# A layer of chunked attention and gated FFN on one core: the first blocks' start, block 1 by seven products, and the order of the head

## The chip, the cores and the metric

The kernel runs on one core of a Trainium2 chip. The core has five engines that this text names by the profile's letters: PE (TensorE, matrix products), DVE (VectorE), ACT (ScalarE), POOL (GpSimd) and SP (SyncE, which here only issues transfers). Matrix products are written to PSUM, which the kernel uses as eight banks of 128 x 512 floats; everything else lives in SBUF. The metric is the device time of one execution in microseconds (us), the median over several runs.

## The reference

The input x is 4 sequences of 2048 tokens of 256 features, 8192 tokens in all. Cut to what matters:

```python
# attention, in chunks of 32 tokens
Q, K, V = x @ W_q.T, x @ W_k.T, x @ W_v.T
S = einsum(Qc, Kc) * mask          # inside each chunk; mask[i, j] = decay**(i-j), i >= j
O = einsum(S, Vc)
a = (sigmoid(x @ W_g.T) * O) @ W_o.T + x
h = layernorm(x + a)
# FFN, weights are integers times 1/127, hidden width 768
f = (silu(h @ wg.T) * (h @ wu.T)) @ wd.T
out = layernorm(h + f)
```

Both layer norms are without weights, with an epsilon of 1e-5.

## The kernel before, in words

**Blocks.** The tokens are worked on in 16 blocks of 512 (`NB`, `TB`). For each block the attention part makes a gate `sg`, a product `y = x M` (with M = W_q^T W_k made once in `make_m`, L188, so that scores need one projection instead of two), values `v`, masked scores `sT`, gated values `goT`, and the output projection plus twice x (the kernel halves wo instead, `HALF`), which is then normalised to `h`. The FFN part makes gate and up products of six chunks of 128 hidden features (`ffn_up`, banks `fg` and `fu`) and the down product (`ffn_down`, bank `fdn`), with each operand split in a high part (fp32r) and a low part (f16). The two parts are software-pipelined: the loop at L934 runs the FFN of block b beside the attention of blocks b+2 and b+3. What comes before that loop, the attention of blocks 0 and 1 and the beginning of block 2, is called the head here (L892 to L922).

**Dense and by sevenths.** A product of the attention part can be made in two ways. The dense way (`attn_gate` L560, `attn_y` L576, `attn_v` L592, and `project_back` L658 under `attn_out` L694) multiplies the whole operands: 8 block products of half size. The other way (`seven`, L482) is a Strassen-type scheme that needs only 7 products of half size, of sums of quarters: products 1, 6, 5 and 7 go to four banks, the additions are made from them by ACT, DVE and POOL, and in a second call (`rest`) products 2, 3 and 4 are accumulated onto the banks of 1, 5 and 7, and the four quarters of the result are put together. The sums of quarters of a weight are made once by POOL (`weight_sums` L423, five operations), those of an activation for each block (`token_sums` L436, four operations; for x, and for `goT` ahead of the output). `split_gate`, `split_v`, `split_y` and `split_out` are the four products in this way. In the kernel before, blocks 2 to 15 use the sevenths (but for the last block's output); blocks 0 and 1 are dense.

**Layer norm.** There are three forms. `layer_norm` (L322) takes the moments (DVE), a square root (ACT, a function that needs another table than the sigmoid), a reciprocal and four normalising operations (DVE). In the loop `scale_and_shift` (L348) and `normalize` (L404) do the last part on ACT, four activations with a scale and a shift. `iterated_scale_and_shift` (L364) has no square root of ACT: three small operations on DVE give a first guess and twelve small ones on POOL improve it; before, only the last blocks use it.

**From h to its transpose.** Block 0's h is transposed on PE (`transpose_h`, L712). For later blocks `move_h` (L731) makes four 32-square transposes on DVE and lets SP issue 16 transfers that put the squares in place, and `split_h` (L754) makes the high and low parts of the result (ACT and POOL) for the next iteration's FFN.

**The order.** The program is written in the order of the Python text, and a scheduler may reorder within an engine; `in_turn`, and `in_steady_turn` inside the loop, keep an operation in its place. Waits follow from the data and from the buffers: most work tiles have two buffers, PSUM has eight banks, and a bank is free again when its reader has read it.

**The start.** At the beginning SP and ACT issue the loads: wg, wv, wk and wo from ACT's queue, the two halves of xT_0, then wq, xT_1, the x blocks and the nine integer pieces of the FFN weights from SP's (`load_w` L129, `load_xT` L117). Meanwhile PE multiplies a tile of zeros (`idle`, L174 to L178), DVE builds the decay mask (L213 to L236), and POOL the identity and zeroed score tiles. Later in the head ACT casts the FFN's integers to their high and low parts (`integers`, L244, 18 casts of 128x512), and DVE finds each piece's largest integer (`look_up`, L260), five pieces in the head and four in iteration 0; a path for wider integers is compiled behind a test and isn't run with these inputs.

The order of the head before:

```python
    sg, v = attn_gate(0), attn_v(0)
    make_m()
    sg_1 = attn_gate(1)
    yT = attn_y(0)
    look_up(range(5))
    v_1 = attn_v(1)
    ...
```

Of the kernel before, what the change touches and what calls it, by code (L numbers as in the profile page):

```python
# [67 lines left out]
WARM = 2  # L68
# [3 lines left out]
def kernel(  # L72
# [36 lines left out]
    def bank(name):  # L109
        return psum.tile([P, TB], F32, tag="ps", name=name)  # L110
# [18 lines left out]
    def load_w(eng, w, name):  # L129
        k, n = w.shape[0] // P, w.shape[1]  # L130
        t = const.tile([P, k, n], w.dtype, tag=name, name=name)
        eng.dma_start(t, w.rearrange("(k p) n -> p k n", p=P))
        return t
# [5 lines left out]
    wg = load_w(nc.scalar, w_gT, "wg")  # L139
# [5 lines left out]
    wo = load_w(nc.scalar, w_oT, "wo")  # L145
# [28 lines left out]
    idle = const.tile([P, TB], F32, tag="idle", name="idle")  # L174
    nc.vector.memset(idle, 0.0)
    pi = bank("pi")
    for _ in range(WARM):
        nc.tensor.matmul(pi, lhsT=idle[:, :P], rhs=idle, start=True, stop=True)  # L178
# [9 lines left out]
    def make_m():  # L188
        pm = bank("pm")
        for ec in range(KD):  # L190
            for dc in range(KD):
                nc.tensor.matmul(
                    pm[:, ec * D : (ec + 1) * D],
                    lhsT=wq[:, dc, ec * P : (ec + 1) * P],
                    rhs=wk[:, dc, :],
                    start=(dc == 0),
                    stop=(dc == KD - 1),
                )
        nc.vector.tensor_copy(m_sb.rearrange("p k n -> p (k n)"), pm)
# [122 lines left out]
    def layer_norm(r, name, on_r=1.0, on_dst=1.0):  # L322


        mv = moments(r, name)
        rstd = root(mv, name, on_r)
        nc.vector.reciprocal(rstd, rstd)
        if on_dst != on_r:
            nc.vector.tensor_scalar(rstd, rstd, on_dst / on_r, None, ALU.mult)
        for g in range(NG):  # L330
            nc.vector.tensor_scalar(
                r[:, g, :],
                r[:, g, :],
                mv[:, g, 0:1],
                rstd[:, g : g + 1],
                ALU.subtract,
                ALU.mult,
            )
# [221 lines left out]
    def attn_gate(b):  # L560
        xt = xTs[b]
        sg = work.tile([P, KD, TB], F32, tag="sg", name=f"sg_{b}")
        for dc in range(KD):
            pg = bank(f"pg_{b}_{dc}")
            for ec in range(KD):
# [6 lines left out]
                )  # L572
            nc.scalar.activation(sg[:, dc, :], pg, AF.Sigmoid)
# [317 lines left out]

    hs, hTs = {}, {}  # L892
    sg, v = attn_gate(0), attn_v(0)
    make_m()
    sg_1 = attn_gate(1)
    yT = attn_y(0)
    look_up(range(5))
    v_1 = attn_v(1)
    in_turn(nc.scalar.mul(wo, wo, HALF))
    fg = integers(ffn_gT, ffn_int[0], "fg")  # L900
    fu = integers(ffn_uT, ffn_int[1], "fu")
    fd = integers(ffn_dT, ffn_int[2], "fd")
    sT = attn_scores(0, yT)
    for w, name in ((wv, "v"), (m_sb, "m"), (wg, "g")):
        w_sums[name] = weight_sums(w, name)
    xTs[2] = load_xT(2)
    x_sums = token_sums(xTs[2], "x_2")
    yT = attn_y(1)
    goT = attn_values(0, sT, v, sg)
    sT_1 = attn_scores(1, yT)  # L910
    w_sums["o"] = weight_sums(wo, "o")
    xTs[3] = load_xT(3)
    hs[0] = attn_out(0, goT)
    v, rest = split_v(2, x_sums)
    goT = attn_values(1, sT_1, v_1, sg_1)
    rest()
    yT, rest = split_y(2, x_sums)
    hs[1] = attn_out(1, goT)
    hTs[0] = transpose_h(0, hs[0])
    rest()  # L920
    sg, g_rest = split_gate(2, x_sums)
# [5 lines left out]
    scales_h = scales_out = r_out = None  # L927
    table = const.tile([P, 1], F32, tag="table", name="table")
# [5 lines left out]
    for b in range(NB - 2):  # L934
# [10 lines left out]
        moving = move_h(b + 1, hs[b + 1])  # L945
# [8 lines left out]
        ffn_up(b, hT, uT, range(2, 3))  # L954
        if not more:
            normalize(r_before, *scales_out)
            store(b - 2, r_before)
# [260 lines left out]
```

## Time and profile before

| quantity | value |
|---|---|
| runs of the kernel before | 533.03, 533.13, 533.16 us (median 533.13) |
| the profiled execution | 532.91 us |
| its span, first to last instruction | 531.1 us |
| granted TensorE clock, mean | 0.996 |
| PE instructions in the span | 3610 matmul records |
| DVE, ACT, POOL busy | 73%, 60%, 62% of the span |
| transfers | 36.90 MB, mean 69 GB/s; 253 GB/s in the first of the 40 slices |

How to read it. The profiled execution is one run, 0.22 us below the median. Its span leaves out 1.8 us around the first and the last instruction. An engine is busy from the start to the end of an instruction; the page puts these together by line and operation, and for the matmuls, which overlap, the end is modelled. A PE stage is best read from the chain of waits, whose pieces follow on one another without overlap: each has a start and a length, then the engine, the bank it writes, the line, and how many records it holds. A 32-bit matmul leaves two records, so 8 records are four matmuls. In the timeline the number in brackets is the idle time just ahead of an instruction on its engine, and after the arrow what ended it.

### The profile page before, as it was taken

How to read it: one execution, taken by the hardware profiler on the slowest of the kernel's cores; microseconds unless marked ns; L12 is line 12 of the kernel's file. 1: busy time of each engine (PE TensorE's matmuls, PEld its weight loads, DVE VectorE, ACT ScalarE, POOL GpSimd, SP SyncE). 2: the span in 40 equal slices, each digit the busy share in tenths (PEclk: the TensorE clock that was granted, in tenths of full speed). 3: DMA queues.
4: the chain of work that ended last, by engine and by line, in shares of the span. 5: the costliest groups of instructions: out<-in, count | busy, mean ns of one | idle time of the engine just before them, and what ended most of it. 6: DMA issues, size and time to landing. Idle time of an engine off the chain costs nothing.

```text
span 531.1 us, 10442 instructions
## 1 busy us (share of the span) xinstructions
PE 518.6 (98%) x3610; PEld 418.4 (79%) x3610; DVE 389.3 (73%) x972; ACT 317.0 (60%) x630; POOL 331.2 (62%) x465
## 2 busy tenths in 40 slices
PE   8999999999999999999999999999999999999983
PEld 5588887887978788887878888788797878877753
DVE  4669787686786867777686777868678686788664
ACT  2284566465656656565576666656565665766553
POOL 5231775667848668585766848577684866644562
PEclk9999999999999999999999999999999999999998
DMA  7541210213212131231313113131221312021111
GB/s 253 184 119 39 51 69 25 58 44 79 79 36 85 52 108 41 51 109 30 92 49 113 42 40 102 37 101 41 61 100 32 89 54 69 1 73 47 41 39 44
DMA packets 43128, 36.90 MB, mean 69 GB/s; under 512 B 4672, under 2 KB 38976, under 8 KB 43072
## 3 DMA queue, kind: packets, MB, share of 16 engines
q1 hardware_dynamic: 41952, 35.15, 22.6%
q10 hardware_dynamic: 1088, 1.05, 0.6%
q8 instruction: 30, 0.49, 0.4%
q14 instruction: 26, 0.21, 0.1%
q0 software_dynamic: 32, 0.00, 0.0%
HBM read 20.45 MB, written 8.39 MB: 54 GB/s over the span
## 4 chain that ended last, share of the span: by engine, by line
PE 91%; DVE 3%; POOL 2%; ACT 2%; issue 1%; DVEq 0%; ACTq 0%
PE fg L781 15%; PE fu L781 14%; PE fdn L668 13%; PE p_v L470 8%; PE p_y L452 8%; PE p_g L452 8%; PE p_o L470 8%; PE po L642 5%; PE ps L621 3%; PE pa L668 2%; PE py L582 1%; PE pg L566 1%; PE pv L601 1%; POOL u_lo L806 1%; PE fdn L1079 1%
## 5 line engine op out<-in xcount | busy, mean ns | idle before, releaser
L806 POOL TENSOR_TENSOR u_lo<-u,u_hi 128x512 f16<-128x512 f32 (+1 forms) x98 | 122.9, 1255 | 117.3 <-ACT u_hi L805 115.7
L805 ACT CAST u_hi<-u 128x512 fp32r<-128x512 f32 (+1 forms) x98 | 59.7, 609 | 65.0 <-DVE u L803 64.7
L791 DVE SCALAR_TENSOR_TENSOR s<-fg,s 128x512 f32<-128x512 f32 (+1 forms) x98 | 66.4, 678 | 37.6 <-ACT s L789 37.2
L789 ACT ACTIVATE s<-fg 128x512 f32<-128x512 f32 (+1 forms) x98 | 56.1, 584 | 40.6 <-PE fg L781 40.5
L803 DVE TENSOR_TENSOR u<-fu,s 128x512 f32<-128x512 f32 (+1 forms) x98 | 66.6, 679 | 11.0 <-POOL u_lo L806 1.0
L781 PE MATMUL fg<-hT_hi,fg_hi 128*128 128x512 f32 (+1 forms) x196 | 74.1, 459 | 0.3 <-DVE s L791 0.3
L781 PE MATMUL fu<-hT_hi,fu_hi 128*128 128x512 f32 (+1 forms) x196 | 60.6, 390 | 0.3 <-DVE u L803 0.3
L781 PE MATMUL fg<-hT_lo,fg_lo 128*128 128x512 f16 (+1 forms) x196 | 57.9, 377 | 0.2 <-DVE s L791 0.2
L781 PE MATMUL fu<-hT_lo,fu_lo 128*128 128x512 f16 (+1 forms) x196 | 57.4, 375 | 0.4 <-DVE u L803 0.4
L668 PE MATMUL fdn<-fd_hi,u_hi 128*128 128x256 f32 x312 | 45.7, 288 | 0.0
L781 PEld LDWEIGHTS fu<-hT_hi,fu_hi 128*128 128x128 f32 x196 | 36.5, 188 | 8.9 <-DVE u L803 0.5
L781 PEld LDWEIGHTS fg<-hT_hi,fg_hi 128*128 128x128 f32 x196 | 34.6, 189 | 9.4 <-DVE s L791 0.5
L407 ACT ACTIVATE h<-h,shift_h,scale_h 128x256 f32<-128x256 f32 x52 | 27.0, 589 | 22.6 <-POOL shift_h L358 22.6
L668 PEld LDWEIGHTS fdn<-fd_hi,u_hi 128*128 128x128 f32 x312 | 38.9, 189 | 0.3
L668 PE MATMUL fdn<-fd_lo,u_lo 128*128 128x256 f16 x312 | 38.6, 273 | 0.0
L781 PEld LDWEIGHTS <-fu_lo 128*128 128x128 f16 x196 | 19.2, 98 | 22.8 <-issue 0.6
L764 POOL TENSOR_TENSOR hT_lo<-hT,hT_hi 128x512 f16<-128x512 f32 x28 | 35.2, 1279 | 1.2 <-ACT hT_hi L763 1.2
L829 DVE SCALAR_TENSOR_TENSOR r<-fdn,h 128x512 f32<-128x512 f32 x30 | 20.7, 689 | 20.6 <-PE fdn L668 18.1
L781 PEld LDWEIGHTS <-fg_lo 128*128 128x128 f16 x196 | 15.3, 98 | 21.3 <-issue 13.3
L668 PEld LDWEIGHTS <-u_lo 128*128 128x128 f16 x312 | 28.5, 98 | 3.9
L642 PE MATMUL po<-sT,v 128*128 128x128 f32 x256 | 31.2, 275 | 0.0
L642 PEld LDWEIGHTS po<-sT,v 128*128 128x128 f32 x256 | 30.0, 192 | 0.6 <-issue 0.5
(202 smaller groups left out, 1159.5 us busy)
## 6 DMA issues: line engine op xcount, KB each, us to landing
x<-in_x_dram SPq DMA_DIRECT2D x16, 512.0 KB, 3.6
xT<-in_xT_dram SPq DMA_DIRECT2D x15, 512.0 KB, 4.3
out_dram<-r SPq DMA_DIRECT2D x15, 512.0 KB, 4.0
hT<-sq SPq DMA_DIRECT2D x224, 32.0 KB, 1.9
fg_int<-in_ffn_gT_dram SPq DMA_DIRECT2D x3, 256.0 KB, 7.9
fu_int<-in_ffn_uT_dram SPq DMA_DIRECT2D x3, 256.0 KB, 7.0
fd_int<-in_ffn_dT_dram SPq DMA_DIRECT2D x3, 256.0 KB, 6.0
xT<-in_xT_dram SPq DMA_DIRECT2D x2, 256.0 KB, 4.2
```

The lines of the kernel that those rows point to most:

```text
L407: nc.scalar.activation(r[:, g, :], r[:, g, :], AF.Identity, bias=shift[:, g : g + 1], scale=scale[:, g : g + 1],)
L452: nc.tensor.matmul(pb, lhsT=a[i - 1], rhs=b[i - 1], start=first, stop=True, skip_group_check=True,)
L470: nc.tensor.matmul(pb[:, g * P : (g + 1) * P], lhsT=b[i - 1][:, g * P : (g + 1) * P], rhs=a[i - 1], start=first and g == 0, stop=True, ski ...
L642: nc.tensor.matmul(po[:, cols], lhsT=v[:, g, dc * P : (dc + 1) * P], rhs=sT[:, cols], start=True, stop=True,)
L668: nc.tensor.matmul(pb[:, j * D : (j + 1) * D], lhsT=part[:, g * P : (g + 1) * P], rhs=w, start=(i == 0), stop=(i == len(terms) - 1),)
L764: nc.gpsimd.tensor_tensor(in_order[1], whole, in_order[0].bitcast(F32), ALU.subtract)
L781: nc.tensor.matmul(pb, lhsT=w[kind][:, dc, hc * P : (hc + 1) * P], rhs=hT[kind][:, dc, cols], start=(kind == kinds[0] and dc == 0), stop=( ...
L789: order(nc.scalar.activation(s, pg, AF.Sigmoid, scale=SCALE / H_UP))
L791: gated = nc.vector.scalar_tensor_tensor(s, pg, U_UP / H_UP**2, s, ALU.mult, ALU.mult)
L803: in_steady_turn(nc.vector.tensor_tensor(u, pu, s, ALU.mult))
L805: nc.scalar.copy(hi, u)
L806: nc.gpsimd.tensor_tensor(lo, u, hi.bitcast(F32), ALU.subtract)
```

## The change

All of it lies in the head and in iteration b = 0; the code of later iterations issues what it issued before.

- Start: wg is loaded in two transfers, one for each half of the contracted dimension, and `attn_gate` runs over that dimension in its outer loop, with both banks open. wo is loaded from SP's queue, after xT_1. The warm-up is seven matmuls of 128x128 in place of two of 128x512, and the zero tile is 128x128.
- Block 1's gate, y, v and output are made by `split_gate`, `split_y`, `split_v` and `split_out`. So POOL makes the weight sums of wg and wv, the sums of x_1, and the sums of M and of wo early, and the sums of block 1's goT for its output. wo is halved earlier.
- M is copied out of PSUM by ACT rather than DVE.
- The casts of the FFN weights stand at three places of the head rather than at one.
- h_1 is scaled by `iterated_scale_and_shift`, and normalised by ACT after chunk 2 of iteration 0; its move follows there, rather than at the start of that iteration.
- The sigmoid's table is asked for by an activation of its own after block 0's transposes. `layer_norm` takes an argument that is not used.

```diff
--- before.py
+++ after.py
@@ -65,7 +65,7 @@
 EPS = 1e-5
 U_UP = 2.0**-3
 HALF = 0.5
-WARM = 2
+WARM = 7
 
 
 @with_exitstack
@@ -126,23 +126,26 @@
         nc.sync.dma_start(xn, x[span(b, start), :].rearrange("(g p) d -> p g d", p=P))
         return xn
 
-    def load_w(eng, w, name):
-        k, n = w.shape[0] // P, w.shape[1]
-        t = const.tile([P, k, n], w.dtype, tag=name, name=name)
-        eng.dma_start(t, w.rearrange("(k p) n -> p k n", p=P))
+    def load_w(eng, w, name, pieces=1):
+        n_k, n = w.shape[0] // P, w.shape[1]
+        t = const.tile([P, n_k, n], w.dtype, tag=name, name=name)
+        src = w.rearrange("(k p) n -> p k n", p=P)
+        per = n_k // pieces
+        for k in range(0, n_k, per):
+            eng.dma_start(t[:, k : k + per, :], src[:, k : k + per, :])
         return t
 
 
     decay = const.tile([P, 1], F32, tag="decay", name="decay")
     nc.gpsimd.dma_start(decay, log_decay[0:1, 0:1].to_broadcast([P, 1]))
     xTs, xns = {}, {}
-    wg = load_w(nc.scalar, w_gT, "wg")
+    wg = load_w(nc.scalar, w_gT, "wg", pieces=KD)
     xTs[0] = load_xT(0, pieces=KD)
     wv = load_w(nc.scalar, w_vT, "wv")
     wq = load_w(nc.sync, w_q, "wq")
     wk = load_w(nc.scalar, w_k, "wk")
     xTs[1] = load_xT(1)
-    wo = load_w(nc.scalar, w_oT, "wo")
+    wo = load_w(nc.sync, w_oT, "wo")
     xns[0] = load_xn(0)
     xns[1] = load_xn(1)
 
@@ -171,11 +174,11 @@
     ]
 
 
-    idle = const.tile([P, TB], F32, tag="idle", name="idle")
+    idle = const.tile([P, P], F32, tag="idle", name="idle")
     nc.vector.memset(idle, 0.0)
-    pi = bank("pi")
+    pi = bank("pi")[:, :P]
     for _ in range(WARM):
-        nc.tensor.matmul(pi, lhsT=idle[:, :P], rhs=idle, start=True, stop=True)
+        nc.tensor.matmul(pi, lhsT=idle, rhs=idle, start=True, stop=True)
 
     ident = const.tile([P, P], F32, tag="ident", name="ident")
     make_identity(nc, ident)
@@ -196,7 +199,7 @@
                     start=(dc == 0),
                     stop=(dc == KD - 1),
                 )
-        nc.vector.tensor_copy(m_sb.rearrange("p k n -> p (k n)"), pm)
+        nc.scalar.copy(m_sb.rearrange("p k n -> p (k n)"), pm)
 
 
 
@@ -319,10 +322,10 @@
         )
         return std
 
-    def layer_norm(r, name, on_r=1.0, on_dst=1.0):
-
-
-        mv = moments(r, name)
+    def layer_norm(r, name, on_r=1.0, on_dst=1.0, mv=None):
+
+
+        mv = moments(r, name) if mv is None else mv
         rstd = root(mv, name, on_r)
         nc.vector.reciprocal(rstd, rstd)
         if on_dst != on_r:
@@ -560,9 +563,9 @@
     def attn_gate(b):
         xt = xTs[b]
         sg = work.tile([P, KD, TB], F32, tag="sg", name=f"sg_{b}")
-        for dc in range(KD):
-            pg = bank(f"pg_{b}_{dc}")
-            for ec in range(KD):
+        banks = [bank(f"pg_{b}_{dc}") for dc in range(KD)]
+        for ec in range(KD):
+            for dc, pg in enumerate(banks):
                 nc.tensor.matmul(
                     pg,
                     lhsT=wg[:, ec, dc * P : (dc + 1) * P],
@@ -570,6 +573,7 @@
                     start=(ec == 0),
                     stop=(ec == KD - 1),
                 )
+        for dc, pg in enumerate(banks):
             nc.scalar.activation(sg[:, dc, :], pg, AF.Sigmoid)
         return sg
 
@@ -889,43 +893,51 @@
 
 
 
+    table = const.tile([P, 1], F32, tag="table", name="table")
     hs, hTs = {}, {}
     sg, v = attn_gate(0), attn_v(0)
+    w_sums["g"] = weight_sums(wg, "g")
+    w_sums["v"] = weight_sums(wv, "v")
+    x_sums = token_sums(xTs[1], "x_1")
     make_m()
-    sg_1 = attn_gate(1)
+    w_sums["m"] = weight_sums(m_sb, "m")
+    in_turn(nc.scalar.mul(wo, wo, HALF))
+    w_sums["o"] = weight_sums(wo, "o")
+    sg_1, g_rest = split_gate(1, x_sums)
+    fg = integers(ffn_gT, ffn_int[0], "fg")
     yT = attn_y(0)
     look_up(range(5))
-    v_1 = attn_v(1)
-    in_turn(nc.scalar.mul(wo, wo, HALF))
-    fg = integers(ffn_gT, ffn_int[0], "fg")
+    g_rest()
+    v_1, rest = split_v(1, x_sums)
     fu = integers(ffn_uT, ffn_int[1], "fu")
+    sT = attn_scores(0, yT)
+    xTs[2] = load_xT(2)
+    rest()
+    yT, rest = split_y(1, x_sums)
+    goT = attn_values(0, sT, v, sg)
+    rest()
     fd = integers(ffn_dT, ffn_int[2], "fd")
-    sT = attn_scores(0, yT)
-    for w, name in ((wv, "v"), (m_sb, "m"), (wg, "g")):
-        w_sums[name] = weight_sums(w, name)
-    xTs[2] = load_xT(2)
+    hs[0] = attn_out(0, goT)
+    sT_1 = attn_scores(1, yT)
+    xTs[3] = load_xT(3)
     x_sums = token_sums(xTs[2], "x_2")
-    yT = attn_y(1)
-    goT = attn_values(0, sT, v, sg)
-    sT_1 = attn_scores(1, yT)
-    w_sums["o"] = weight_sums(wo, "o")
-    xTs[3] = load_xT(3)
-    hs[0] = attn_out(0, goT)
     v, rest = split_v(2, x_sums)
     goT = attn_values(1, sT_1, v_1, sg_1)
+    go_sums = token_sums(goT, "go_1")
     rest()
     yT, rest = split_y(2, x_sums)
-    hs[1] = attn_out(1, goT)
+    hs[1], out_rest = split_out(1, go_sums)
     hTs[0] = transpose_h(0, hs[0])
+    in_turn(nc.scalar.activation(table, eps, AF.Sigmoid))
     rest()
+    scales_h = iterated_scale_and_shift(out_rest(), of_h, "h_1")
     sg, g_rest = split_gate(2, x_sums)
     ahead = yT, v, sg
 
 
 
 
-    scales_h = scales_out = r_out = None
-    table = const.tile([P, 1], F32, tag="table", name="table")
+    scales_out = r_out = None
 
     def back_to_sigmoids():
 
@@ -942,7 +954,7 @@
         steady = b > 0
         if b:
             normalize(hs[b + 1], *scales_h)
-        moving = move_h(b + 1, hs[b + 1])
+            moving = move_h(b + 1, hs[b + 1])
         ffn_up(b, hT, uT, range(0, 1))
         if b == 0:
             g_rest()
@@ -952,6 +964,10 @@
         if m + 1 < NB:
             xTs[m + 1] = load_xT(m + 1)
         ffn_up(b, hT, uT, range(2, 3))
+        if b == 0:
+
+            normalize(hs[b + 1], *scales_h)
+            moving = move_h(b + 1, hs[b + 1])
         if not more:
             normalize(r_before, *scales_out)
             store(b - 2, r_before)
```

## The prediction

> **What bounds the kernel now.** I read the page first: busy shares, slices, the chain that ended last.
>
> ```profile
> PE 518.6 (98%) x3610; PEld 418.4 (79%) x3610; DVE 389.3 (73%) x972; ACT 317.0 (60%) x630; POOL 331.2 (62%) x465
> PE   8999999999999999999999999999999999999983
> PE 91%; DVE 3%; POOL 2%; ACT 2%; issue 1%; DVEq 0%; ACTq 0%
> ```
>
> TensorE is busy 98% of the span; only the first slice and the last two fall short. So the time is the sum of the matmuls plus the start and the tail. The change touches only the head, so I asked for PE's waits in the first 85 us.
>
> ```profile
> PE pi L178 <- DVE idle L175: 1.5, 1, 1.5
> ```
>
> That is the only one, before the warm-up. After it no matmul of the head waits: a matmul removed here is a matmul saved, and a new wait costs in full. The chain of waits of the first 80 us prices each stage (start, length):
>
> ```profile
> 1.46 3.58 PE pi L178 x4
> 5.04 0.02 issue
> 5.06 3.70 PE pg L566 x8
> ...
> 12.22 1.73 PE pm L192 x8
> 13.94 3.43 PE pg L566 x8
> 17.38 3.51 PE py L582 x8
> 20.89 3.45 PE pv L601 x16
> 24.34 1.08 PE ps L621 x32
> 25.42 3.63 PE py L582 x8
> ...
> 42.21 3.45 PE pa L668 x16
> ...
> 47.83 1.73 PE p_g L452 x8
> ...
> 51.36 1.29 PE p_g L452 x6
> ...
> 57.53 1.78 PE p_v L470 x16
> ...
> 61.11 1.34 PE p_v L470 x12
> ```
>
> The reader sees a dense stage at about 3.44 us (the second py shows 3.63, behind the narrow score products; I take 3.44 for it as for the others) beside the same stage by sevenths: 1.73 + 1.29 = 3.02 where tokens stay in the columns (gate, y) and 1.78 + 1.34 = 3.12 where they are rows (v, out). The start, from the timeline (start, length, engine; in brackets the idle time and what ended it):
>
> ```profile
> 5.06 0.30 PEld L566 LDWEIGHTS pg<-xT,wg 128*128 128x128 f32 x2 [1.40 <-DMA wg<-in_w_gT_dram]
> ```
>
> The first real matmul waited for wg. The answer on DMA issues (queue, KB, us to landing):
>
> ```profile
> wg<-in_w_gT_dram ACTq DMA_DIRECT2D x1, 256.0 KB, 4.3
> ```
>
> Issued at 0.74, wg landed at 5.04; the first half of xT_0, issued at 0.75, took 3.7 and landed at 4.45.
>
> [...] passes of 128x512 take 0.86 us from 1.46 to 5.04 and 0.43 soon after. [...]
>
> **The change part by part.** Changed lines of DVE, ACT and POOL count only where PE comes to wait for them, and the order from iteration 0 on is the old one, so what the head gains or loses reaches the end one to one.
>
> Sevenths for block 1. Gate 3.43 − 3.02 = 0.41; y 3.44 − 3.02 = 0.42; v 3.45 − 3.12 = 0.33; out 3.45 − 3.12 = 0.33. Sum −1.49 us. Into the bargain, py's 0.07 above 3.44 (it waited a little for m_sb behind DVE's 16 mask copies, 13.43 to 16.41) goes, since ACT, idle there, copies m_sb about 2 us earlier: −0.07.
>
> Start. wg in halves with the ec loop outside lets two matmuls begin on half of wg and half of xT_0. The half of wg is not in the trace; bounds are 5.04 (no gain) and 4.45, below which xT_0 holds it up. I take 4.47, as half of the bytes come first in an otherwise idle queue: 5.06 − 4.47 = −0.59. The warm-up must not be in the way: 7 matmuls are 14 passes of 0.86 / 4 = 0.215, 3.0 us; from about 1.12 (the memset is a quarter of 0.48) to 4.15. Before, it ended only at 5.04, so undoing the load alone would give nothing.
>
> Clock. If the full clock comes at the same moment as now (about 5.1), the 0.6 us of matmul begun early run at half speed and 0.3 is given back; if it comes with activity, nothing. The warm-up also ends 0.3 before work begins. I take +0.1 (0 to 0.3).
>
> wv. It is now third in ACT's DMA queue instead of second. On each queue the third load of before moved nothing until about 2.1 us after the first had landed; if that is a matter of loads, wv lands at 7.6 to 8.7, if of bytes at 6.5 as before. The v matmuls want it at 4.47 + 3.5 = 8.0: 0 to 0.7, I take +0.2. wk (fourth, wanted at 11.4, 9.55 before) and wo (on SP, landing near 12.1, halved by ACT and wanted by POOL after 14) have room.
>
> New waits. I laid the new order of each engine on the durations of the trace. PE order after the gate of block 0: v, m, four gate products of block 1 (13.3), y of block 0, three gate products, four v products, scores of block 0, and so on.
> - Gate products 6, 5, 7 need POOL's x_1 sums: xT_1 lands at 11.43, three sums of 0.73 end near 13.7, product 6 is due at 13.7: 0 to 0.2, I take 0.
> - The last v product of block 1 needs p57_v from DVE, which stands behind five top reduces of 0.62 = 3.1 us begun near 19.4 and block 0's mask products; due 23.95, free about 24.1: +0.15 (0 to 0.5). Behind the waiting product stand the y products.
> - Values of block 1 need their masked scores while DVE still normalises h_0 (1.38): +0.1 (0 to 0.4).
> - Output of block 1: goT comes late from DVE for the same reason, then POOL makes three sums of 0.73 = 2.2 us; PE has 1.34 + 1.73 + 0.44 = 3.5 us to cover goT and sums: +0.25 (0 to 0.9).
> - x_3 sums on POOL stand behind the rooting by iteration. Its price is in the tail of before, which does the same:
>
> ```profile
> 488.57 0.20 POOL L371 TENSOR_TENSOR t_out<-y_out 128x4 f32<-128x4 f32 x1 [0.39 <-DVE y_out L389]
> 488.85 0.20 POOL L371 TENSOR_TENSOR t_out<-t_out,v_out 128x4 f32<-128x4 f32 x1
> ```
>
>   one step each 0.28, eleven dependent ones 3.0 us. The v products of block 3 come three FFN chunks later: +0.1 (0 to 0.6).
> - In iteration 0 ACT normalises h_1 after chunk 2, as in the later loop:
>
> ```profile
> 83.21 2.08 ACT L407 ACTIVATE h<-h,shift_h,scale_h 128x256 f32<-128x256 f32 x4 [2.05 <-POOL shift_h L358]
> 51.16 1.42 DVE L739 STREAM_TRANSPOSE sq<-h 128x256 f32<-128x256 f32 x4
> ```
>
>   2.08 us on ACT ahead of the sigmoid of chunk 3, and the four transposes stop DVE until it is done. Cover on PE is the four v products and chunk 3's 1.8 us; slack about 0.2. I take 0 (0 to 0.95).
> Sum of waits +0.6 (0 to about 3.3).
>
> Hidden at no cost. Layer norm's four DVE operations for h_1 (1.38) go, covered before by PE anyway. Casts in three pieces are the same 18 x 0.55 us of ACT; fg comes first at block 0's y, fd only before the out stage, and FFN wants all near 49, so there are over 5 us left. The table loads are as many (two). SP: hT_1 is moved some 7 us later; its 16 DMAs took 11.4 + 1.9 us, so it lands near 74.7 and PE wants its split near 80.4; if that cover went, each us late would cost one. What is late next when the dense matmuls go is DVE and POOL in block 1's head, which is the list above.
>
> Sum: −1.49 − 0.07 − 0.59 + 0.1 + 0.2 + 0.6 = −1.25. From the profiled execution's 532.91 us (span 531.1 and 1.8 around it) that gives 531.66; the median of the runs is 533.13, 0.22 above the profiled one, so 531.9.
>
> **Rivals.** Times are on the median's scale.
> - A, forecast: 531.9 (531.3 to 532.4 by the mid values).
> - D, all hidden: waits, clock and wv at nothing: 533.13 − 2.15 = 531.0. For it: no wait at all in the head of before. Against: DVE's five reduces sit in the way.
> - B, given back: the start gains nothing, for instance since wg's first half or the clock come as late as now (+0.6), wv costs 0.7 and the waits 0.9: −1.56 + 1.6, 533.1. [...] This is also the case in which the change does not do what it says: the load in halves starts nothing earlier.
> - C, slower: the chain in iteration 0. POOL's 3.0 us of rooting delays the normalise, ACT's 2.08 delay the sigmoid, DVE stands at the transposes, and PE runs out of free banks at chunk 3. Price: 2.08 + 1.42 less 0.2 of slack, 3.3 us; from 531.9 to 535.2, and some 534.7 if half a us is hidden. It decides from a wait of 1.25 us on over no change, and of 2.3 on for a clear loss. For it: three engines in series with a slack of 0.2. Against: the later iterations carry the same normalise at their start, and the longest single wait of PE on another engine after the head is 0.5 us.
>
> **How the numbers follow.** Chances: A 0.42, D 0.15, B 0.25, C 0.18. A measurement tells about 0.2% (1.07 us) from no change. Faster by more: all of D and 0.35 of A, 0.50. Within: 0.07 of A and 0.23 of B, 0.30. Slower: C and 0.02 of B, 0.20. The range for 8 in 10 runs from D's near end, 530.8, into C, 534.5; A's own is 531.3 to 532.4.
>
> **What would show it.** In the changed trace: the first pg near 4.47 and the warm-up over by 4.2; the pg passes at 0.43 from about 5.1; the first pv right behind pg; block 1's stages at 3.0 to 3.1 us each; PE waits for x_sums, p57_v, go_sums of some tenths; and none at chunk 3 of iteration 0. Wrong would make it: a first pg at 5.0, a gap ahead of pv, or a PE wait over 1 us with ACT's normalise or POOL's rooting behind it.

## The result, and the profile after

The changed kernel takes 533.59 us (median of 22 runs, 532.94 to 535.15). Beside it the kernel before was run 22 times and has a median of 532.53 us (531.59 to 533.26), so the three runs shown ahead of the change were on the high side of its spread. The ratio is 1.0021, with a 95% interval of 1.0014 to 1.0027: the change makes the kernel 1.1 us slower. The forecast was 1.25 us faster.

The page of the changed kernel shows the same picture as before, a full PE. The columns are busy time, share and instructions of each engine.

```profile
PE 520.6 (98%) x3656; PEld 425.3 (80%) x3656; DVE 395.3 (74%) x981; ACT 322.4 (61%) x644; POOL 344.7 (65%) x492
PE   8999999999999999999999999999999999999985
```

PE is busy 2.0 us longer than before although the edits take 1.5 us of matmuls out. The head's waits of PE, after the change, for 0 to 90 us (total, times, longest):

```profile
PE pi L181 <- DVE idle L178: 1.1, 1, 1.1
PE p_o L473 <- POOL go_sums L446: 0.8, 1, 0.8
PE pv L605 <- DMA wv<-in_w_vT_dram: 0.6, 1, 0.6
PE p_v L473 <- DVE p_v L508: 0.3, 1, 0.3
PE p_g L455 <- DVE p_g L508: 0.2, 1, 0.2
```

There were none below the first line before. To see where the time goes, the run is cut at points that both kernels have: the first matmul of M, the first of the FFN, the last operation of DVE, the end. First PE's timeline of the kernel before (start, length; the length overlaps the next line by some 0.15):

```profile
12.05 1.89 PE L192 MATMUL pm<-wk,wq 128*128 128x256 f32 x8
...
49.21 0.81 PE L781 MATMUL fg<-hT_hi,fg_hi 128*128 128x512 f32 x2
```

and of the kernel after:

```profile
4.21 4.21 PE L569 MATMUL pg<-xT,wg 128*128 128x512 f32 x8
9.03 3.72 PE L605 MATMUL pv<-wv,xT 128*128 128x256 f32 x16 [0.62 <-DMA wv<-in_w_vT_dram]
12.59 1.89 PE L195 MATMUL pm<-wk,wq 128*128 128x256 f32 x8
...
20.71 0.67 PE L455 MATMUL p_g<-x_sums,g_sums 128*128 128x256 f32 x2 [0.20 <-DVE p_g L508]
...
26.10 0.71 PE L473 MATMUL p_v<-v_sums,x_sums 128*128 128x128 f32 x4 [0.34 <-DVE p_v L508]
...
43.82 1.60 PE L473 MATMUL p_o<-o_sums,go_sums 128*128 128x128 f32 x12 [0.81 <-POOL go_sums L446]
...
50.31 0.81 PE L785 MATMUL fg<-hT_hi,fg_hi 128*128 128x512 f32 x2
```

The last DVE operation starts at 524.87 before and 527.34 after; the spans are 531.1 and 531.4.

| stretch | before | after | difference |
|---|---|---|---|
| start to the first matmul of M | 12.05 | 12.59 | +0.54 |
| to the first FFN matmul | 37.16 | 37.72 | +0.56 |
| to the last DVE operation | 475.66 | 477.03 | +1.37 |
| to the end | 6.19 | 4.09 | −2.10 |

Four things, then, where the prediction had one sum: the start lost time although PE began 0.85 us earlier; the head lost time although it has 1.5 us less to multiply; the loop, in which no instruction was changed after iteration 0, lost 1.4; and the last stores were quicker. The profiled run of before lay 0.4 above its median and that of after 0.4 below, so the spans of the traces differ by 0.4 and the medians by 1.06.

The loop's share is in one stage. The down product of block 1 in the chain of waits (start, length), first before, then after:

```profile
108.91 5.43 PE fdn L668 x48
```

```profile
110.13 5.53 PE fdn L672 x48
```

In the iteration laid side by side stage for stage (from 181 us on) no other stage differs by more than 0.01. The groups by form, 80 to 470 us, give the mean of one in ns after the comma, first before, then after:

```profile
L668 PE MATMUL fdn<-fd_hi,u_hi 128*128 128x256 f32 x298 | 43.8, 288 | 0.0
L668 PE MATMUL fdn<-fd_lo,u_lo 128*128 128x256 f16 x300 | 37.1, 273 | 0.0
```

```profile
L672 PE MATMUL fdn<-fd_hi,u_hi 128*128 128x256 f32 x306 | 45.9, 292 | 0.0
L672 PE MATMUL fdn<-fd_lo,u_lo 128*128 128x256 f16 x302 | 37.5, 273 | 0.0
```

Each high part takes 4 ns longer, the low parts take the same. With 24 high parts in a block that is 0.09 us, in 14 iterations 1.3 us. No wait shows there: it is the matmul itself. What had moved is where the operands lie: the change allocates `table`, 4 bytes in a slot of 32, ahead of the FFN's weights instead of behind them. So fd_hi, a multiple of 64 bytes into the partition before, is 32 bytes past one after. The instructions of the loop and their order are the same. Another difference between the two traces can be set aside: the changed kernel's has 3.4 us at half clock near the end (from 517.3 us), but a second trace of it without that, e13 below, takes 477.00 us from the first FFN matmul to the last DVE operation, where this one takes 477.03.

The head's delays begin on DVE. The 16 mask copies, before (from the timeline of DVE):

```profile
13.43 2.98 DVE L236 COPY mask<-chunk_mask 32x32 f32<-32x32 f32 x16
```

and after:

```profile
14.67 5.10 DVE L239 COPY mask<-chunk_mask 32x32 f32<-32x32 f32 x16
```

They are the same copies, 0.19 apart before and 0.32 after. POOL was idle from 11.0 to 17.2 before; after, it makes the sums of x_1, M and wo between 11.4 and 19.5, with a pause of 0.8 us. The mask is finished 3.4 us later, and the additions of block 1's gate, y of block 0, the five top reduces and the additions of block 1's v all stand behind it in DVE's order.

The start and the head are therefore not two separate sums. In e13, the changed kernel run once more, wv came later still and M began at 13.64 instead of 12.59; but PE then met DVE's additions ready, the waits at p_g and p_v were gone, and the first FFN matmul began at the same 50.31.

### The profile page after: what moved, and what is told of

It is laid out like the page before. It is cut to its first block, busy times and chain, and to the rows that moved or that the text cites. A ratio compares the mean times of both kernels' runs of the same rounds, so it can differ in the third digit from the quotient of the medians.

```text
span 531.4 us, 10605 instructions
## 1 busy us (share of the span) xinstructions
PE 520.6 (98%) x3656; PEld 425.3 (80%) x3656; DVE 395.3 (74%) x981; ACT 322.4 (61%) x644; POOL 344.7 (65%) x492
## 4 chain that ended last, share of the span: by engine, by line
PE 86%; DVE 7%; POOL 2%; ACT 2%; issue 1%; DMA 1%; DVEq 0%; ACTq 0%; POOLq 0%
PE fg L785 15%; PE fu L785 14%; PE fdn L672 14%; PE p_o L473 8%; PE p_y L455 8%; PE p_v L473 8%; PE p_g L455 8%; PE po L646 5%; PE ps L625 3%; PE pa L672 1%; DMA decay<-in_log_decay_dram 1%; POOL u_lo L810 1%; PE fdn L1095 1%; DVE mask L239 1%; ACT r L410 1%
## 5 line engine op out<-in xcount | busy, mean ns | idle before, releaser
L672 PE MATMUL fdn<-fd_hi,u_hi 128*128 128x256 f32 x312 | 46.9, 292 | 0.0
L473 PE MATMUL p_v<-v_sums,x_sums 128*128 128x128 f32 x240 | 31.8, 275 | 0.3 <-DVE p_v L508 0.3
```

What stands on the lines that cost most here:

```text
L473: nc.tensor.matmul(pb[:, g * P : (g + 1) * P], lhsT=b[i - 1][:, g * P : (g + 1) * P], rhs=a[i - 1], start=first and g == 0, stop=True, ski ...
L672: nc.tensor.matmul(pb[:, j * D : (j + 1) * D], lhsT=part[:, g * P : (g + 1) * P], rhs=w, start=(i == 0), stop=(i == len(terms) - 1),)
```

## Experiments

Several kernels were run on different chips, each with the kernel before beside it; its median there was 532.52 (e1 to e4), 532.92 (e5 to e8), 532.40 (e9 to e12), 533.02 (e13 to e16) and 532.50 (e17). Runs of different groups are compared by their ratio to it or by stretches of their traces, not by their medians.

### Memory places: e1, e2, e16, e17

e1_aligned: the changed kernel with

```diff
     table = const.tile([P, 1], F32, tag="table", name="table")
+    const.tile([P, 8], F32, tag="pad_0", name="pad_0")
 ...
     fd = integers(ffn_dT, ffn_int[2], "fd")
+    const.tile([P, 8], F32, tag="pad_1", name="pad_1")
```

> The changed kernel with two unused 32-byte tiles, one behind the sigmoid-table tile and one behind the FFN weights, so that the FFN's weight tiles start at a multiple of 64 bytes again as before the change (they stand at 32 past one in the changed kernel), and all later tiles too; instruction order is the same on every engine. Theory P (place): the down product's high part takes 0.09 us longer per iteration (5.52 against 5.43) because its moving operand starts at an odd multiple of 32 bytes; then each fdn stage reads 5.43 here and the time is 1.2 us below the changed kernel's 533.6, near 532.4. Rival (the chip or the run): fdn stays at 5.5 or varies, and the time stays at 533.6.

532.37 us, ratio to before 1.0002 (0.9994 to 1.0010).

e2_before_table: the kernel before with

```diff
+    table = const.tile([P, 1], F32, tag="table", name="table")
     hs, hTs = {}, {}
 ...
     scales_h = scales_out = r_out = None
-    table = const.tile([P, 1], F32, tag="table", name="table")
```

> The kernel before with only the sigmoid-table tile allocated ahead of the head, so that the FFN's weight tiles start 32 bytes past a multiple of 64; the order of instructions is that of the kernel before on every engine. Theory P: fdn 5.52 per iteration in place of 5.43, 1.2 us slower than before (533.7 against 532.5). Rival: no change (532.5).

533.65 us, ratio 1.0026 (1.0016 to 1.0037). The stage of block 1 in the chains of waits, e1 and then e2:

```profile
110.40 5.43 PE fdn L672 x48
```

```profile
108.91 5.53 PE fdn L668 x48
```

The reader sees the two lengths change places with the 32 bytes: about 1.2 us come and go with one tile's slot, in both kernels. This is shown, not argued.

Which operand minds it? e16_hT_shift has only pad_0, so that fd_hi (the moving operand of fdn) is on a multiple of 64 and u_hi (its stationary one) and hT_hi are not.

> The changed kernel with one 32-byte pad, behind the sigmoid-table tile: the FFN weights stand at multiples of 64 bytes as in e1_aligned, but every later tile (hT and its parts, u, x) at 32 past one. Theory P2 (it is the moving operand of a one-pass fp32r product that must start at a multiple of 64 bytes): fdn, whose moving operand is the weight, is back at 5.43, and the high parts of fg and fu, whose moving operand is hT_hi, get longer by about 4 ns a matmul, 24 of them, 0.1 us per iteration; so the iterations stay at 31.69 and the time near the changed kernel's. Rival (it is the weights' place as such): iterations of 31.60, 1.2 us less.

533.44 us, ratio 1.0010 (1.0002 to 1.0019), no different from the changed kernel's 1.0009 on the same chip (e13); and e17_both_shift, which has only pad_1:

> The changed kernel with one 32-byte pad, behind the FFN weights: the down product's moving operand (fd_hi) and its stationary one (u_hi) both start 32 bytes past a multiple of 64. Measured so far: both at multiples of 64, fdn 5.43; one of them shifted, either one, 5.52. Theory E (each shifted operand costs): 5.52 or more here, up to 5.61, iterations of 31.69 or more. Rival (only a difference between the two costs): 5.43, iterations of 31.60, and the time 1.2 us below the changed kernel's.

532.48 us, ratio 0.9998 (0.9989 to 1.0007). Again the chains, e16 and then e17:

```profile
110.38 5.51 PE fdn L672 x48
```

```profile
110.94 5.43 PE fdn L672 x48
```

The places, as the addresses in the built programs give them (bytes past a multiple of 64), beside the mean of one high part of fdn:

| kernel | fd_hi (moving) | u_hi (stationary) | ns |
|---|---|---|---|
| before, e1 | 0 | 0 | 288 |
| after, e2 | 32 | 0 | 292 |
| e16 | 0 | 32 | 292 |
| e17 | 32 | 32 | 288 |

With both operands shifted the stage is as short as with neither; with one shifted, either one, it is longer. Both theories of a preferred place are out (in e16 the high parts of fg, whose moving operand was shifted, kept their 466 ns), and the rival of e17 holds: what costs is that the two operands of the product begin in different halves of 64 bytes. All nineteen traces of this document agree: from the first FFN matmul to the last DVE operation they take 475.65 to 475.95 us where the two halves are the same (twelve traces), and 476.85 to 477.03 where they differ (seven). The low parts of fdn (f16) have the same mismatch in the changed kernel and take 273 ns in all; fg and fu, with moving operands of 512, have it too and don't mind it (466 ns and 394 to 395 in all six). Why only the high parts of fdn do wasn't tried.

### The start: e3, e4, e9, e13, e14, e15

e3_wg_whole undoes the halves of wg; e4_warm_long undoes the warm-up:

```diff
-    wg = load_w(nc.scalar, w_gT, "wg", pieces=KD)
+    wg = load_w(nc.scalar, w_gT, "wg")
```

> The changed kernel with wg loaded in one transfer, all else kept (short warm-up too). Theory S (the start costs more than it gives): first gate matmul near 5.05, the v matmuls start near 8.6 to 8.8 without a wait for wv, which lands near 6.5; the m stage starts 0.3 to 0.5 us earlier than in the changed kernel (12.59 there) and the time is 0.3 to 0.5 us lower. Rival (the early start is a gain): the m stage starts 0.3 to 0.8 later and the time is so much higher.

> The changed kernel with the old warm-up of two 128x512 matmuls, wg still in halves. The warm-up then ends near 5.04 and the gate starts there rather than at 4.21. Theory S: wv sets the v stage (start 9.0, as in the changed kernel), so the time stays within 0.2 us of the changed kernel's. Rival (the early start is what counts): 0.6 to 0.8 us slower. If the short warm-up is what delayed the full clock (0.6 us later in the changed kernel's trace), the clock rises near 4.7 here.

e3: 532.60 us, ratio 1.0001 (0.9992 to 1.0009), 1.0 less than the changed kernel, more than expected. e4: 533.95, ratio 1.0029 (1.0017 to 1.0041), 0.4 above the changed kernel and between the two expectations; full clock came at 6.4 and not at 4.7, so a long warm-up doesn't secure an early step. In e3 the gate starts at 4.53, since wg as a whole landed by then (in the trace of the kernel before it landed at 5.04, just when the warm-up ended), and the v stage follows without a wait:

```profile
8.34 3.62 PE L605 MATMUL pv<-wv,xT 128*128 128x256 f32 x16
```

So by these two traces (4.53 against 4.21) the halves bring 0.3 us and make wv the third load of ACT's queue. The answer on DMA issues of the changed kernel (KB, us to landing):

```profile
wg<-in_w_gT_dram ACTq DMA_DIRECT2D x2, 128.0 KB, 3.6
...
wv<-in_w_vT_dram ACTq DMA_DIRECT2D x1, 256.0 KB, 7.3
```

Issued at 1.67 it lands at 9.0 (9.6 in e1, 10.1 in e13, the changed kernel again, 533.41 us with 1.26 us of wait for wv). As the second load it took 5.3 before. e13 was run as a reference for the next three:

> The changed kernel, unaltered, on the chip of the next three runs, to have them beside it. As first measured: 1.0 to 1.1 us above before.

Its ratio is 1.0009 (1.0000 to 1.0017), on a chip where before has 533.02: the change loses some 0.5 us there, half of what was expected. What makes the chips differ was not looked into.

e14_wv_on_sp puts wv second on SP's queue and leaves the halves:

```diff
-    xTs[0] = load_xT(0, pieces=KD)
-    wv = load_w(nc.scalar, w_vT, "wv")
+    xTs[0] = load_xT(0)
+    wv = load_w(nc.sync, w_vT, "wv")
```

> The changed kernel with wv as the second load of SP's queue and xT_0 in one transfer as its first; wg stays in halves, first and second on ACT's queue. Theory Q (the third load of a queue starts late, whatever its size): wv lands near 6 to 6.5 instead of 9.0 to 9.6, the v stage starts right behind the gate, 0.3 to 1.2 us less than the changed kernel; the gate may start up to 0.5 later, with xT_0 whole. Rival (bytes in flight decide): wv still lands at 8 or later, no gain.

wv took 4.8 us and PE didn't wait for it. It was fast as the second load behind 512 KB, and slow as the third behind 256 KB (7.3 in the changed kernel's trace), and e3, where PE didn't wait for wv either, has the same 256 KB of wg ahead of wv on the same queue as the changed kernel, in one load instead of two: in these traces it went with the place in the queue (4.7 to 5.3 us as the second load, 7.3 to 8.4 as the third), not with the bytes ahead. In all traces the third load of either queue took 6.9 to 9.1 us; why is not known. Yet the time is 534.02 (ratio 1.0017, 1.0010 to 1.0023), no gain: xT_0 as a whole came at 5.07, 0.65 us after the warm-up had ended, and the gate then ran at half speed for 4 us. That is the third piece of the start. e9_before_short gave the kernel before the short warm-up alone (`WARM = 7`, 128x128), and e15_before_gap one of four matmuls:

```diff
-WARM = 2
+WARM = 4
-    idle = const.tile([P, TB], F32, tag="idle", name="idle")
+    idle = const.tile([P, P], F32, tag="idle", name="idle")
```

> The kernel before with only the warm-up of the change: seven 128x128 matmuls of zeros in place of two of 128x512, so that PE stands idle from about 4.1 us until wg has landed (4.4 to 5.1). Theory W (the idle stretch can make the clock miss its step: in e5 to e8 the idle time was 0.6 to 0.8 us and full clock came at 9.3 to 10.4, in e3 it was 0.4 and full clock came at 5.1): some runs about 2.3 us slower than others, the slow ones at 534 to 535; where wg is early the start is up to 0.5 earlier and the run near 532.0. Rival (the moment of full clock is chance, whatever the warm-up): the spread of the runs is that of the kernel before, about 2 us, around the same median.

> The kernel before with four 128x128 matmuls of zeros, over near 2.8 us, so that PE always stands idle for 1.6 us or more ahead of the gate. Theory W (a stretch of idle time defers full clock): full clock at 8 us or later, the m stage 0.8 to 2.4 us later than the 12.0 of before, and the median 1 to 2 us above before. Rival (only when the phase is right, the idle time does not matter): full clock between 4.7 and 7.1 as in the other runs and the median within 0.5 us of before.

e9: 532.45 us, ratio 0.9998 (0.9990 to 1.0006), one group of runs, so the slow ones that theory W expected didn't come; the idle time was 0.21 in its trace, too short to tell. e15: 535.06 us, ratio 1.0032 (1.0020 to 1.0045). Its gate, in PE's timeline:

```profile
5.12 5.50 PE L566 MATMUL pg<-xT,wg 128*128 128x512 f32 x8 [1.99 <-DMA wg<-in_w_gT_dram]
```

The same eight records took 3.70 before. The step of the granted clock (the start of the first record at full clock in each trace; the matmuls' starts go from 0.86 to 0.43 us apart at the same moment), beside the idle time ahead of the gate as the timeline gives it (for e3 that is 0.1, from 4.42 to 4.53, and not the 0.4 of e9's expectation):

| idle ahead of the gate | full clock from (us), one trace each |
|---|---|
| none (long warm-up: before, e2, e4, e10, e11, e12) | 4.7, 5.2, 6.4, 5.6, 7.1, 5.3 |
| up to 0.21 (after, e1, e3, e9, e13, e16, e17) | 5.3, 4.2, 5.1, 6.0, 5.7, 4.2, 6.2 |
| 0.57 to 0.76 (e5 to e8, e14) | 9.9, 10.4, 9.3, 10.4, 9.0 |
| 1.99 (e15) | 8.8 |

In the six traces with 0.57 us or more of idle time between the zeros and the gate, full clock came at 8.8 us or later; in the thirteen with 0.21 us or less it came by 7.1. Within a row the moment differs by up to 2.4 us, and what sets it was not shown. A step 2.4 us later costs 1.2 us, by an estimate from the 0.86 and 0.43 us above, so much of the spread of 1.7 us between runs of one kernel can come from it. The chip is not the reason for the late steps: e13 and e16 ran on the same one as e14 and e15. The changed kernel's warm-up is over at 4.2 to 4.4 and leaves no cover when wg is late.

### The waits of the head: e5 to e8 and e10 to e12

e5_base is the changed kernel with both repairs, and e10_old_start the same with the old warm-up. Two theories were tried on them, on e5 each alone (e6 for N, e7 for D) and both together (e8), on e10 D (e11) and both (e12): N, block 0's layer norm is in the way of block 1's goT on DVE; D, POOL slows DVE. N's edit, then D's (`order` passes to each of the five operations of `weight_sums`):

```diff
-    hs[0] = attn_out(0, goT)
+    hs[0] = attn_residual(0, goT)
 ...
     goT = attn_values(1, sT_1, v_1, sg_1)
+    layer_norm(hs[0], "a0", on_r=HALF, on_dst=H_UP)
```

```diff
-    w_sums["m"] = weight_sums(m_sb, "m")
-    w_sums["o"] = weight_sums(wo, "o")
     sg_1, g_rest = split_gate(1, x_sums)
+    w_sums["m"] = weight_sums(m_sb, "m", in_turn)
 ...
     fd = integers(ffn_dT, ffn_int[2], "fd")
+    w_sums["o"] = weight_sums(wo, "o", in_turn)
```

> The changed kernel with wg in one transfer (as in e3_wg_whole) and the FFN weights at multiples of 64 bytes (as in e1_aligned). If the two effects are separate they add: 533.6 - 1.0 - 1.2 = 531.4, v stage without a wait, iterations of 31.60 us. If they share something (the same slack, the same tail): 532.0 to 532.4. It is also what the next three runs are compared with.

> e5_base with block 0's layer norm written after block 1's gated values, so that DVE makes the second goT of block 1 before the four normalising operations of h_0. Theory N (goT behind the normalising operations is what makes the output products wait for go_sums): the wait of p_o on go_sums (0.8) goes, and the time is 0.8 to 1.1 us below e5_base. Rival (POOL's chain of three sums is too long anyway): the wait shrinks by less than 0.3 and the time stays.

> e5_base with POOL's weight sums of M moved behind its sum for block 1's gate and those of wo behind its sum for block 1's y, so that POOL is idle while DVE builds the mask (from about 14 us on). PE and DVE keep their order. Theory D (DVE is slowed by POOL beside it: the 32x32 mask copies are 0.33 us apart against 0.19 in the kernel before, where POOL was idle then): the copies are 0.19 apart, the mask is done 1.5 to 2 us earlier, the waits of p_g (0.2) and p_v (0.3) on DVE go, time 0.5 to 0.9 us below e5_base. Rival (the five top reduces are what delays p_v, whenever they start): the p_v wait stays and the time changes by less than 0.2.

> e6_norm_late and e7_pool_late together. If both theories hold: 1.3 to 2.0 us below e5_base, near 529.6, with no wait of PE over 0.2 us in the first 85 us after the warm-up. If a next wait takes over: less than the sum of the two.

Measured: 532.56, 532.39, 532.33 and 532.38 us, ratios 0.9992 (0.9985 to 1.0000), 0.9987 (0.9979 to 0.9995), 0.9976 (0.9964 to 0.9988) and 0.9979 (0.9967 to 0.9990). All gain less than expected (e5 lies 0.4 below before, where the two repairs in sum would give 1.1), and none of the four settles its question by its time: on this chip wg landed at 5.0 to 5.2, all four profiles have the late clock, and the runs of e7 fall into two groups (530.3 to 530.9 and 531.7 to 534.3), as do those of e8. The late clock also takes away what D's edit is to mend: M begins at 14.46 in e5, POOL is idle while the mask is copied and the copies are 0.19 apart already; from M to the first FFN matmul e5 and e7 both take 36.67 us. N's edit does show in the traces: e6 takes 36.13. The gate of e5:

```profile
5.13 6.03 PE L569 MATMUL pg<-xT,wg 128*128 128x512 f32 x8 [0.72 <-DMA wg<-in_w_gT_dram]
11.00 3.62 PE L605 MATMUL pv<-wv,xT 128*128 128x256 f32 x16
```

With the old warm-up in place of the gap:

> e5_base with the old warm-up, so that start and memory places are those of the kernel before and what is left of the change is block 1 by sevenths, the casts, the rooting by iteration and the order. Theory W: clock near 5, none of the runs has the late clock, m stage near 12.0; the head from the m stage to the first FFN product takes 37.2 to 37.7 (37.2 before, 37.7 in the changed kernel), since the matmuls saved come back as waits; with the last stores' tail 1.7 shorter than before's the time is 531.0 to 531.6. Rival (sevenths alone are a gain of 1.5): the head takes 35.6, time below 530.

> e10_old_start with POOL's sums moved as in e7. With full clock early the mask is wanted early: theory D gives mask copies 0.19 apart, no p_g wait and no p_v wait, 0.5 to 0.9 us less than e10. Rival: less than 0.2.

> e10_old_start with POOL's sums moved and block 0's layer norm after block 1's gated values. Theory N adds 0.5 to 1.0 to what e11 gives, time 529.3 to 530.2 in all runs (the late clock of e5 to e8 is gone). If a late clock still comes, the runs fall in two groups again, 530 and 532.4.

| run | us, ratio to before (95%) | M starts at | M to FFN in the trace |
|---|---|---|---|
| e10 | 532.33, 0.9994 (0.9986 to 1.0002) | 12.22 | 37.11 |
| e11 | 532.02, 0.9984 (0.9975 to 0.9994) | 12.97 | 36.67 |
| e12 | 531.57, 0.9983 (0.9975 to 0.9992) | 12.06 | 36.14 |

e10 says what block 1 by sevenths is worth by itself: the head takes 37.11 us where it took 37.16, and the time can't be told from before (it was expected at 531.0 to 531.6). The 1.5 us of matmuls were all given back. e11 shows what theory D says of DVE: the mask copies of e10, then of e11,

```profile
13.54 5.25 DVE L239 COPY mask<-chunk_mask 32x32 f32<-32x32 f32 x16
```

```profile
13.70 3.38 DVE L239 COPY mask<-chunk_mask 32x32 f32<-32x32 f32 x16
```

are 0.33 apart beside POOL and 0.21 almost without it (POOL's sums of x_1 end at 14.26). Over all traces they are 0.31 to 0.35 apart where POOL makes the sums of M and wo beside them (eight) and 0.19 to 0.21 where it doesn't (eleven). By what means POOL slows DVE the traces do not show. The head of e11 is 0.44 shorter and the p_v wait is gone, but its M starts 0.75 later than e10's, and e13 loses the wait by a later start alone, without D's edit (36.67, too). e12 settles it, for there M starts earlier than in e10. The product that waits for p_v, e10 and then e12:

```profile
25.11 0.71 PE L473 MATMUL p_v<-v_sums,x_sums 128*128 128x128 f32 x4 [0.17 <-DVE p_v L508]
```

```profile
24.63 0.61 PE L473 MATMUL p_v<-v_sums,x_sums 128*128 128x128 f32 x4
```

Of the 0.97 us by which e12's head is shorter than e10's, N's part is 0.53 (from e11 to e12; 0.54 from e5 to e6), half of what it claimed, and the 0.44 left are D's (a little under the 0.5 expected). By the times alone e11 and e12 can't be told apart. Of the waits of PE in the head only one is left in e12:

```profile
PE p_o L473 <- DVE v L529: 0.3, 1, 0.3
```

e12 beats both kernels: by the ratios it is 0.9 us under before and 1.4 to 2.0 under the changed kernel. It misses its expectation of 529.3 to 530.2, though, and its runs spread over 2.3 us (530.11 to 532.42); the profiled one is the fastest. In its trace full clock came at 5.3; whether a later clock makes the longer runs can't be told from their times.

## Why the prediction was wrong

By stretches, the forecast had −0.3 us for the start (−0.59 + 0.1 + 0.2), −1.0 for the head (−1.49 − 0.07 + 0.6) and nothing for the loop and the tail. The traces have +0.54, +0.56, +1.37 and −2.10. The two largest losses that the forecast missed are the head's waits, too small by 1.5, and the loop, which was taken to be unchanged; the start missed 0.8, and the tail, which wasn't in the sum, hides most of this in these two traces. Point by point, by its own steps:

- **Sevenths, −1.49.** The stages are as long as predicted (p_g 1.73, p_v 1.34 and so on), and where the operands were ready the saving came; so did py's 0.07 (the stage took 3.44). Right in kind and size.
- **Start, −0.59.** The first gate matmul began at 4.21, earlier than the 4.47 that was taken. But 0.59 is not what the halves bring. In the trace of before, wg's landing and the end of the warm-up fell together at 5.04, and a whole wg takes 3.7 to 4.4 us from run to run: in e3 the gate began at 4.53, in e9, with the short warm-up alone, at 4.62. In such a run the short warm-up alone brings most of the gain and the halves 0.3; where wg is as late as in e5 to e8 they may bring more, which no run shows.
- **Clock, +0.1 (0 to 0.3).** The gate took 4.20 rather than 3.54 to the next stage: +0.66. Full clock came 0.6 later than in the trace of before (5.3 against 4.7), and the matmuls of the first 1.1 us ran at half speed. The range, up to 0.3, was less than half of that, and that the short warm-up could leave idle time and push the step to 9 us wasn't seen at all.
- **wv, +0.2 (0 to 0.7).** 0.62 of wait in the profiled run, 0.7 to 1.7 in the other traces with the halves and the short warm-up (e1, e13, e16, e17). Of the two readings offered, loads and bytes, it was loads (e14); its landing, given as 7.6 to 8.7, was 9.0 to 10.1. The start in sum: −0.85 earlier, +0.66 clock, +0.62 wv and 0.11 in the v stage, +0.54.
- **Waits, +0.6 (0 to 3.3).** The places were right: p_v behind the top reduces, 0.34 against 0.15; go_sums 0.81 against 0.25; the gate 0.20 against 0, though it waited for DVE's additions behind the mask and not for POOL's x_1 sums. Iteration 0's chain cost nothing, as said, and the x_3 sums, taken at 0.1, neither: from 52 to 90 us PE waits for nothing, though ACT's normalise stands there,

```profile
61.38 2.08 ACT L410 ACTIVATE h<-h,term_h,y_h 128x256 f32<-128x256 f32 x4
```

  so rival C fell. The sizes were too small for two reasons. DVE's durations were taken from a trace in which POOL was idle; beside POOL they are longer (mask 5.10 for 2.98, block 0's four normalising operations 2.02 for 1.37). And a wait cost more than the idle time that the profile gives, in which the ends of matmuls are modelled: the stage behind it starts 0.97 late at go_sums where the idle time is 0.81, 0.50 for 0.34 at p_v, 0.37 for 0.20 at p_g. That makes 1.84; the head's loss against the sum of matmuls is 37.72 − (37.16 − 1.56) = 2.12, and 0.3 of it has no place in the trace.
- **"The order from iteration 0 on is the old one, so what the head gains or loses reaches the end one to one."** This step failed outright, and it is the one that e1 and e2 settle. The order was the old one, but not the memory: 1.3 us were lost in a loop that issues the same instructions. No rival had it.
- **The tail** wasn't in the sum either. The last four stores took, before and then after,

```profile
out_dram<-r SPq DMA_DIRECT2D x4, 128.0 KB, 3.1
```

```profile
out_dram<-r SPq DMA_DIRECT2D x4, 128.0 KB, 1.7
```

  and the end came 2.1 us sooner behind the last DVE operation. Four traces of the program before have 5.7 to 6.2 us there, the traces of the changed one 4.1 to 5.4. In the former, three transfers of instructions start 0.8 to 1.8 us after the last DVE operation does, beside the last stores; in the latter, one. That these delay the stores was not tested. The tail also moves with edits that have nothing to do with it: e5 and e10 differ in the warm-up alone, and have 4.1 and 5.3 us. An untested term of this size is a reason not to read gains under 1 us from the times alone.

Without the memory place and with the start of before, the change is worth nothing (e10): rival B, "given back", was the nearest. Its 0.7 for wv was about right, its 0.9 for the waits still too small (1.35 of idle time, 1.84 of delay).

## What to carry to other kernels

Where PE is full, count not only instructions but the address of each tile: a tile allocated earlier shifts all later ones, and two operands of one product in different halves of 64 bytes cost this kernel 1.2 us, as much as all the edits were meant to bring. Durations of DVE hold only for the neighbour they were measured beside: work given to POOL was paid on DVE as well here, in mask copies (5.10 us for 2.98) and normalising operations (2.02 for 1.37). A stretch that starts later can be shorter for that alone (the head took 36.67 us in e13, 37.72 in the first trace of the same kernel), so compare two heads only when they start alike. And the warm-up that reached to the first real product was worth more here as a bridge than the few tenths that its shortening may free: with 1.99 us between the two (e15) full clock came at 8.8 us, and the ratio to before was 1.0032.

## What the runs showed of the hardware

- The high parts of the down product (fp32r, 128x256) take 292 ns against 288 when stationary and moving operand differ by 32 bytes modulo 64, whichever of them is shifted, and 288 when both are. The 128x512 products of the same kind (466 ns for fg) and the f16 ones (273 ns) are the same in all.
- Full clock came between 4.2 and 7.1 us in thirteen traces in which PE was busy from 1.1 or 1.5 us with at most 0.21 us of pause, and between 8.8 and 10.4 in six with a pause of 0.57 us or more.
- DVE's 32x32 copies stood 0.31 to 0.35 us apart beside POOL's sums of M and wo, 0.19 to 0.21 without them.
- wv, 256 KB, landed 7.3 to 8.4 us after its issue as the third load of ACT's queue, and 4.7 to 5.3 as the second of either queue. Between the two the DMA engines move as little as 0 to 21 GB/s (0.2 us slices from 4.6 to 5.2 us of the changed kernel's trace).
